# Half of a feed-forward stage's features turned by DMA transposes as pairs of float16 numbers, and 1/std taken for two groups at once

## The chip, the cores and the metric

The kernel runs on one core of a Trainium2 chip. The metric is the device time of one execution in microseconds (us), the median of three runs. A separate, profiled execution gives the page and the trace that are quoted below. Engines: PE is TensorE (PEld its weight loads), DVE is VectorE, ACT is ScalarE, POOL is GpSimd, SP issues transfers.

## The reference

Two layers, each a graph attention followed by a feed-forward part, each with a residual, on x of 4096 x 256 float32 and one 4096 x 4096 adjacency matrix. The change touches the feed-forward part of layer 0 alone, a recurrence of 30 steps on the 4096 rows:

```python
def step(h, _):
    h = h + 0.01 * jnp.tanh(h)
    h = h * jax.nn.sigmoid(h)
    h = _layernorm(h, ln_w, ln_b)
    h = jnp.einsum('bsc,dc->bsd', h, W) + b
    return (h, None)
x, _ = jax.lax.scan(step, x, None, length=N_ITERS)      # N_ITERS = 30
...
x = x + _L0_ffn_ref((_layernorm(x, axis=-1))[None], ...)[0]
```

W is 256 x 256. Each row is independent of the others, so different rows may stand in different steps at the same time, but a row's step needs the result of its step before.

## The kernel before, in words

The kernel is written in a tile framework: the program states operations and the pools from which their buffers come, and the framework puts the operations of each engine into a queue whose order it chooses, and adds the semaphore waits. An engine works through its queue strictly in that order. Stages: attention 0 (to about 842 us), the feed-forward recurrence (842 to about 1921 us), attention 1 with its two layers, a router, and a mixture of experts.

In the feed-forward stage all 4096 rows stay on chip in `y` (128 partitions x 32 row tiles x 256 columns, float32). `y` holds 100 times h, which spares a multiplication. A group is four row tiles (G = 4, 512 rows); there are eight groups (NG = 8). A unit is one group in one step, so there are 30 x 8 = 240 units, and unit u + 8 is the next step of unit u's group. The loop over `at` starts unit `at` and carries earlier units on, so that several are under way:

- unit `at`: L739, ACT, `th = tanh(0.01 y)`, 128 x 1024; L740, POOL, `th = th + y`.
- unit `at - 1`: L745, ACT, `z = silu(0.01 th)`. Then `over_std` (L101 to L106): the row statistics on DVE (four of L101, four of L103), the addition of EPS (L105, DVE) and the power -0.5 (L106, POOL) give 1/std of each row.
- unit `at - 2`: L114, PE, eight transposes of `z` by 128 x 128 into PSUM (`tp`), then L780, ACT, a copy to SBUF (`zT`, 128 x 1024).
- unit `at - 3`: L754, PE, eight float32 products of `zT` with `wT` (W transposed, the layer norm's weight and mean folded in) into `po`; each float32 product is two records in the trace. Then L764, DVE, four times `y = po * (1/std) + bias`.

```python
th[at] = work.tile([P, G, C], F32, name="th")
nc.scalar.activation(th[at], y[:, g * G : (g + 1) * G, :], AF.Tanh, scale=0.01)
nc.gpsimd.tensor_tensor(th[at], th[at], y[:, g * G : (g + 1) * G, :], OP.add)
...
z = zs[at - 1] = work.tile([P, G, C], F32, name="z", bufs=4)
nc.scalar.activation(z, th.pop(at - 1), AF.Silu, scale=0.01)
rs[at - 1] = over_std(small, z)[0]
...
zT[at - 2] = work.tile([P, KC, GR], F32, name="zT")
nc.scalar.copy(zT[at - 2], pt)
```

`th` and `zT` have three buffers each (the pool `f_work`), `z` has four, `po` and `tp` two each in PSUM. In the last step (units 232 to 239) L764 adds `last` in place of `bias`, and L774, DVE, adds the residual. Before the loop, `init` (L679 to L683) normalizes each group of the stage's input, and a preparation (L698 to L721) makes `wT` and `bias`.

Of the kernel before, what the change touches and what calls it, by code (L numbers as in the profile page):

```python
# [11 lines left out]
F32 = mybir.dt.float32  # L12
BF16 = mybir.dt.bfloat16
F16 = mybir.dt.float16
I32 = mybir.dt.int32
AF = mybir.ActivationFunctionType
OP = mybir.AluOpType
AX = mybir.AxisListType
# [3 lines left out]
P = 128  # L22
C = 256
KC = C // P
# [3 lines left out]
G = 4  # L28
EPS = 1e-5
# [6 lines left out]
TINY = 1e-30  # L36
# [8 lines left out]
def gnn_ffn_kernel(ctx: ExitStack, tc: tile.TileContext, a: dict, out: bass.AP):  # L45
    nc = tc.nc
# [3 lines left out]
    NG = NT // G  # L50
    GR = G * P
# [14 lines left out]
    nc.gpsimd.memset(ones, 1.0)  # L66
    lnscale = const.tile([P, 1], F32, name="lnscale")
    nc.gpsimd.memset(lnscale, math.log(SCALE * LOW))
    mhalf = const.tile([P, G], F32, name="mhalf")
    nc.gpsimd.memset(mhalf, -0.5)  # L70


# [23 lines left out]
    def over_std(pool, src):  # L96

        st = pool.tile([P, G, 6], F32, name="ln_st")
        mv = pool.tile([P, G, 2], F32, name="ln_mv")
        for r in range(G):  # L100
            nc.vector.bn_stats(st[:, r, :], src[:, r, :])  # L101
        for r in range(G):
            nc.vector.bn_aggr(mv[:, r, :], st[:, r, :])  # L103
        rstd = pool.tile([P, G], F32, name="ln_rstd")
        nc.vector.tensor_scalar(rstd, mv[:, :, 1], EPS, None, op0=OP.add)  # L105
        nc.gpsimd.tensor_tensor(rstd, rstd, mhalf, OP.pow)  # L106
        return rstd, mv

    def transposed(psum, src, name="tp"):

        ps = psum.tile([P, KC, GR], F32, name=name)
        for k in range(KC):
            for r in range(G):
                nc.tensor.transpose(ps[:, k, r * P : (r + 1) * P], src[:, r, k * P : (k + 1) * P], ident)  # L114
        return ps
# [540 lines left out]

    with ExitStack() as scope:
        one = scope.enter_context(tc.tile_pool(name="f_one", bufs=1))  # L660
        wT = one.tile([P, KC, C], F32, name="wT")
        bias = one.tile([P, C], F32, name="bias")
        last = one.tile([P, C], F32, name="last")
        y = one.tile([P, NT, C], F32, name="y")
        work = scope.enter_context(tc.tile_pool(name="f_work", bufs=3))
        small = scope.enter_context(tc.tile_pool(name="f_small", bufs=6))

        x1 = {}

        def load(g):  # L670
            if g not in ahead:
                load_ahead(x1d, g)
            x1[g] = ahead.pop(g)

        def init(g):
            t = x1.pop(g)
            rstd, mv = over_std(small, t)
            rs = small.tile([P, G], F32, name="rs")
            nc.vector.tensor_scalar(rs, rstd, 100.0, None, op0=OP.mult)  # L679
            nm = small.tile([P, G], F32, name="nm")  # L680
            nc.vector.scalar_tensor_tensor(nm, mv[:, :, 0], -1.0, rs, op0=OP.mult, op1=OP.mult)
            for r in range(G):
                nc.scalar.activation(  # L683
                    y[:, g * G + r, :], t[:, r, :], AF.Identity, scale=rs[:, r : r + 1], bias=nm[:, r : r + 1]
                )

        load(0)
        load(1)
        with tc.tile_pool(name="f_prep", bufs=1) as prep, tc.tile_pool(name="f_pps", bufs=1, space=PSUM) as pps:
            ln = prep.tile([2 * KC, P], F32, name="ln")  # L690
            nc.scalar.dma_start(ln[:KC], a["L0_ffn_ln_w"].rearrange("(k p) -> k p", p=P))
            nc.scalar.dma_start(ln[KC:], a["L0_ffn_ln_b"].rearrange("(k p) -> k p", p=P))
            wr = prep.tile([P, KC, C], F32, name="wr")
            nc.scalar.dma_start(wr, a["L0_ffn_W"].rearrange("(k p) c -> p k c", p=P))
            nc.scalar.dma_start(bias, bcast_rows(a["L0_ffn_b"]))
            init(0)
            ps = pps.tile([P, 2 * KC], F32, name="ps_ln")
            nc.tensor.transpose(ps, ln, ident[: 2 * KC, : 2 * KC])  # L698
            lnT = prep.tile([P, 2 * KC], F32, name="lnT")
            nc.vector.tensor_scalar(lnT, ps, 100.0, None, op0=OP.mult)  # L700
            lbb = prep.tile([P, KC, P], F32, name="lbb")
            nc.vector.tensor_copy(lbb, lnT[:, KC:, None].to_broadcast([P, KC, P]))
            ps = pps.tile([P, KC, C], F32, name="ps_w")
            for k in range(KC):
                for o in range(KC):
                    nc.tensor.transpose(ps[:, k, o * P : (o + 1) * P], wr[:, o, k * P : (k + 1) * P], ident)
            raw = prep.tile([P, KC, C], F32, name="raw")
            nc.vector.tensor_copy(raw, ps)
            ps = pps.tile([P, C], F32, name="ps_b")
            for k in range(KC):  # L710
                nc.tensor.matmul(ps, lbb[:, k, :], raw[:, k, :], start=(k == 0), stop=(k == KC - 1))
            nc.vector.scalar_tensor_tensor(bias, bias, 100.0, ps, op0=OP.mult, op1=OP.add)

            nc.vector.tensor_scalar(last, bias, -100.0, None, op0=OP.add)
            for k in range(KC):
                nc.vector.tensor_scalar(raw[:, k, :], raw[:, k, :], lnT[:, k : k + 1], None, op0=OP.mult)
            ps = pps.tile([P, C], F32, name="ps_m")
            for k in range(KC):
                nc.tensor.matmul(ps, mean, raw[:, k, :], start=(k == 0), stop=(k == KC - 1))
            for k in range(KC):  # L720
                nc.vector.tensor_tensor(wT[:, k, :], raw[:, k, :], ps, OP.subtract)  # L721

        ps_t = scope.enter_context(tc.tile_pool(name="f_pst", bufs=2, space=PSUM))
        ps_o = scope.enter_context(tc.tile_pool(name="f_pso", bufs=2, space=PSUM))

        th, zs, rs, zT = {}, {}, {}, {}
        units = FFN_STEPS * NG
        for at in range(units + 4):
            if at < NG:
                if at + 2 < NG:  # L730
                    load(at + 2)
                if at:
                    init(at)
            if units - NG <= at - 1 < units:
                load((at - 1) % NG)
            if at < units:
                g = at % NG
                th[at] = work.tile([P, G, C], F32, name="th")
                nc.scalar.activation(th[at], y[:, g * G : (g + 1) * G, :], AF.Tanh, scale=0.01)  # L739
                nc.gpsimd.tensor_tensor(th[at], th[at], y[:, g * G : (g + 1) * G, :], OP.add)  # L740
            if 0 <= at - 2 < units:
                pt = transposed(ps_t, zs.pop(at - 2))
            if 0 <= at - 1 < units:
                z = zs[at - 1] = work.tile([P, G, C], F32, name="z", bufs=4)
                nc.scalar.activation(z, th.pop(at - 1), AF.Silu, scale=0.01)  # L745
                rs[at - 1] = over_std(small, z)[0]
            if 0 <= at - 3 < units:
                u = at - 3
                g = u % NG
                src = zT.pop(u)  # L750
                po = ps_o.tile([P, G, C], F32, name="po")
                for r in range(G):
                    for k in range(KC):
                        nc.tensor.matmul(  # L754
                            po[:, r, :],
                            src[:, k, r * P : (r + 1) * P],
                            wT[:, k, :],
                            start=(k == 0),
                            stop=(k == KC - 1),
                        )  # L760
                rstd = rs.pop(u)
                end = u >= units - NG
                for r in range(G):
                    nc.vector.scalar_tensor_tensor(  # L764
                        y[:, g * G + r, :],
                        po[:, r, :],
                        rstd[:, r : r + 1],
                        last if end else bias,
                        op0=OP.mult,
                        op1=OP.add,  # L770
                    )
                if end:
                    t = x1.pop(g)
                    nc.vector.scalar_tensor_tensor(  # L774
                        t, y[:, g * G : (g + 1) * G, :], 0.01, t, op0=OP.mult, op1=OP.add
                    )
                    nc.sync.dma_start(rows_of(x2d, g), t)
            if 0 <= at - 2 < units:
                zT[at - 2] = work.tile([P, KC, GR], F32, name="zT")
                nc.scalar.copy(zT[at - 2], pt)  # L780


# [457 lines left out]
```

## Time and profile before

| | before |
|---|---|
| median of 3 runs | 3596.79 us (3593.67 to 3600.78) |
| profiled execution, span | 3585.3 us |
| PE busy in the span | 3265.5 us (91%) |
| DVE, ACT, POOL busy | 3013.9 (84%), 2612.6 (73%), 1101.1 (31%) |
| L740, the add on POOL | 240 times, mean 2367 ns |
| L739, L745, tanh and silu on ACT | 240 times each, means 1047 and 1060 ns |
| L780, the copy of zT on ACT | 240 times, mean 1012 ns |
| L764, the update of y on DVE | 928 times, mean 468 ns, and 32 in the last step |
| L106, the power on POOL | 272 times, mean 1040 ns |

The page lists, by line of the kernel, an engine's operations with what they write and read, how often, busy time, and the mean length of one. A line of the timeline gives the start in us, the time from the first start to the last end of operations of one kind in a row, the engine, the line, the operation, its output and inputs with their sizes, how many, and in brackets how long the engine stood idle before it and what it waited for. Lengths overlap: the next operation of an engine can start a little before the last one's end, so that costs in a chain are better read from start to start. In the windows each engine has its busy time and, in parentheses, the number of its instructions. PEclk is the granted clock of PE as a share of its full speed.

### The profile page before, as it was taken

How to read it: one execution, taken by the hardware profiler on the slowest of the kernel's cores; microseconds unless marked ns; L12 is line 12 of the kernel's file. 1: busy time of each engine (PE TensorE's matmuls, PEld its weight loads, DVE VectorE, ACT ScalarE, POOL GpSimd, SP SyncE). 2: the span in 40 equal slices, each digit the busy share in tenths (PEclk: the TensorE clock that was granted, in tenths of full speed). 3: DMA queues.
4: the chain of work that ended last, by engine and by line, in shares of the span. 5: the costliest groups of instructions: out<-in, count | busy, mean ns of one | idle time of the engine just before them, and what ended most of it. 6: DMA issues, size and time to landing. Idle time of an engine off the chain costs nothing. (4 is left out here: it accounts for less than half of the span.)

```text
span 3585.3 us, 80790 instructions
## 1 busy us (share of the span) xinstructions
PE 3265.5 (91%) x33523; PEld 2971.2 (83%) x33523; DVE 3013.9 (84%) x6039; ACT 2612.6 (73%) x2902; POOL 1101.1 (31%) x899
## 2 busy tenths in 40 slices
PE   6789999987999999999998899999979999996895
PEld 5688888886888888888887799999868999994784
DVE  6789999987877877877787799999989999997445
ACT  2688888896766666666663799999879999993221
POOL 3210010003877777777772000000000000001663
PEclk8899999998999999999999899999999999998897
DMA  6796877601000000000006021303130331404224
GB/s 136 138 230 118 204 171 152 191 22 54 7 1 1 1 1 1 1 1 1 1 1 213 19 73 68 116 25 116 56 123 26 121 117 37 131 20 165 82 94 183
DMA packets 280199, 288.46 MB, mean 80 GB/s; under 512 B 97149, under 2 KB 230426, under 8 KB 279834
## 3 DMA queue, kind: packets, MB, share of 16 engines
q1 hardware_dynamic: 198770, 224.18, 18.9%
q0 software_dynamic: 73920, 52.97, 9.6%
q10 hardware_dynamic: 7144, 6.16, 0.6%
q8 instruction: 264, 4.33, 0.5%
q14 instruction: 101, 0.83, 0.1%
HBM read 248.01 MB, written 68.81 MB: 88 GB/s over the span
## 5 line engine op out<-in xcount | busy, mean ns | idle before, releaser
L546 PE MATMUL acc<-vals,m 128*128 128x130 f16 (+1 forms) x19456 | 1723.4, 233 | 138.1 <-DVE u L475 81.8
L466 ACT ACTIVATE st<-f1b,f2b 128x1024 bf16<-128x1024 f32 (+2 forms) x1664 | 1658.5, 1072 | 146.1 <-DVE m L580 138.2
L546 PEld LDWEIGHTS <-m 128*128 128x128 bf16 x19456 | 1525.2, 98 | 232.2 <-issue 85.7
L580 DVE TENSOR_TENSOR m<-st,m 128x2048 bf16<-128x2048 bf16 (+2 forms) x832 | 929.3, 1134 | 16.3 <-ACT st L466 12.4
L754 PE MATMUL po<-wT,zT 128*128 128x256 f32 x3840 | 875.2, 381 | 12.7 <-ACT zT L780 12.3
L754 PEld LDWEIGHTS po<-wT,zT 128*128 128x128 f32 x3840 | 714.0, 191 | 103.9 <-ACT zT L780 14.8
L740 POOL TENSOR_TENSOR th<-th,y 128x1024 f32<-128x1024 f32 x240 | 567.9, 2367 | 194.1 <-ACT th L739 193.5
L546 PE MATMUL acc<-vals,rows 128*128 128x130 f16 x5120 | 611.1, 221 | 0.0
L106 POOL TENSOR_TENSOR ln_rstd<-ln_rstd,mhalf 128x4 f32<-128x4 f32 x272 | 282.5, 1040 | 896.4 <-DVE ln_rstd L105 685.8
L101 DVE BATCH_NORM_STATS2 ln_st<-z 128x6 f32<-128x256 f32 x960 | 337.7, 413 | 191.3 <-ACT z L745 191.3
L546 PEld LDWEIGHTS <-rows 128*128 128x128 bf16 x5120 | 490.8, 96 | 0.4
L780 ACT COPY zT<-tp 128x1024 f32<-128x1024 f32 x240 | 243.0, 1012 | 323.8 <-PE tp L114 323.8
L604 DVE TENSOR_TENSOR rows<-m,m 128x2048 bf16<-128x2048 bf16 x320 | 391.7, 1224 | 10.2
L764 DVE SCALAR_TENSOR_TENSOR y<-po,ln_rstd,bias 128x256 f32<-128x256 f32 x928 | 378.2, 468 | 4.9 <-PE po L754 4.9
L745 ACT ACTIVATE z<-th 128x1024 f32<-128x1024 f32 x240 | 254.3, 1060 | 18.1 <-POOL th L740 17.8
L114 PE MATMUL tp<-ident,z 128*128 128x128 f32 x1920 | 250.8, 274 | 9.0 <-ACT z L745 8.0
L114 PEld LDWEIGHTS tp<-ident,z 128*128 128x128 f32 x1920 | 225.6, 141 | 35.7 <-ACT z L745 10.7
L739 ACT ACTIVATE th<-y 128x1024 f32<-128x1024 f32 x240 | 251.1, 1047 | 4.7 <-DVE y L764 4.7
L209 POOL DMA_DIRECT2D rows<-in_adj_dram x80 | 72.9, 912 | 510.1 <-PE tp_m L219 499.8
L604 DVE TENSOR_TENSOR m<-m,m 128x1792 bf16<-128x1792 bf16 (+1 forms) x200 | 202.2, 1011 | 12.7
L449 POOL MEMSET hs<- 128x4 f32 x3 | 0.3, 101 | 617.6 <-DVE u L490 596.4
L307 PE MATMUL ph<-g_w,xT 128*128 128x264 f32 x384 | 117.5, 469 | 31.1 <-DVE v L377 27.9
(212 smaller groups left out, 2312.9 us busy)
## 6 DMA issues: line engine op xcount, KB each, us to landing
m<-edges SPq DMA_DIRECT2D x32, 2048.0 KB, 9.8
rows<-in_adj_dram POOLq DMA_DIRECT2D x64, 448.0 KB, 7.1
edges<-ms SPq DMA_DIRECT2D x64, 448.0 KB, 5.1
m<-edges SPq DMA_DIRECT2D x16, 1792.0 KB
f1b<-fd SPq DMA_DIRECT2D x32, 512.0 KB, 3.5
rows<-x1d SPq DMA_DIRECT2D x16, 512.0 KB, 6.8
y<-yd SPq DMA_DIRECT2D x16, 512.0 KB, 9.0
f1b<-fd SPq DMA_DIRECT2D x16, 448.0 KB, 3.7
```

Of the source, the lines that this page charges most:

```text
L101: nc.vector.bn_stats(st[:, r, :], src[:, r, :])
L106: nc.gpsimd.tensor_tensor(rstd, rstd, mhalf, OP.pow)
L114: nc.tensor.transpose(ps[:, k, r * P : (r + 1) * P], src[:, r, k * P : (k + 1) * P], ident)
L466: nc.scalar.activation(st[:, s, :w], f1b[c, h][:, :w], AF.Relu, bias=f2b[:, 2 * q + s, h : h + 1], scale=BIG)
L546: nc.tensor.matmul(acc[:, i, cols], lhs[:, s, rows], v[:, cols], start=(j == 0 and n_ == 0), stop=(j == NT - 1 and n_ == 1), skip_group_ch ...
L580: nc.vector.tensor_tensor(m1[:, :, :w], st[:, :, :w], m, OP.logical_and if turned(q) else OP.min)
L604: nc.vector.tensor_tensor(m2[:, :, :w], m, m1[:, :, :w], OP.subtract)
L739: nc.scalar.activation(th[at], y[:, g * G : (g + 1) * G, :], AF.Tanh, scale=0.01)
L740: nc.gpsimd.tensor_tensor(th[at], th[at], y[:, g * G : (g + 1) * G, :], OP.add)
L745: nc.scalar.activation(z, th.pop(at - 1), AF.Silu, scale=0.01)
L754: nc.tensor.matmul(po[:, r, :], src[:, k, r * P : (r + 1) * P], wT[:, k, :], start=(k == 0), stop=(k == KC - 1),)
L764: nc.vector.scalar_tensor_tensor(y[:, g * G + r, :], po[:, r, :], rstd[:, r : r + 1], last if end else bias, op0=OP.mult, op1=OP.add,)
```

## The change

The features of a row are 256 columns. Their first half stays as it was: four transposes on PE instead of eight, a copy by ACT of half the size, four float32 products. The second half takes another way. It is scaled by a power of two and split into two float16 numbers, `z16[:, 0]` (rounded, by ACT) and `z16[:, 1]` (what the rounding lost, by DVE); both are turned by one DMA transpose of 128 x 1024 float16 numbers, issued on SP, into `zT16`; and each part is multiplied with two float16 parts of W's second half, `w16`, which makes four products of 128 x 256 per row tile, added up in PSUM with the float32 product. The scales come from the weights and the bias in the preparation; `under` takes them out again. 1/std is taken for two units at once: the statistics of an even and an odd unit go to one tile `mv2`, and one EPS addition, one power and one multiplication with `under` serve both. The products and the update of y move from `at - 3` to `at - 4`; `zT` and the new tiles have four buffers. It is for relieving PE: fewer float32 products and transposes.

The diff, without the preparation of the scales (some twelve small operations on DVE, one power on POOL, and two products on PE, between L721 and the loop), and without the moved load of the last step:

```diff
-        wT = one.tile([P, KC, C], F32, name="wT")
+        wT = one.tile([P, C], F32, name="wT")
+        w16 = one.tile([P, 2, C], F16, name="w16")
+        scale = one.tile([P, 2], F32, name="scale")
+        under = one.tile([P, 2 * G], F32, name="under")
...
             if 0 <= at - 2 < units:
-                pt = transposed(ps_t, zs.pop(at - 2))
+                z = zs.pop(at - 2)
+                pt = ps_t.tile([P, GR], F32, name="tp")
+                for r in range(G):
+                    nc.tensor.transpose(pt[:, r * P : (r + 1) * P], z[:, r, :P], ident)
             if 0 <= at - 1 < units:
-                z = zs[at - 1] = work.tile([P, G, C], F32, name="z", bufs=4)
-                nc.scalar.activation(z, th.pop(at - 1), AF.Silu, scale=0.01)
-                rs[at - 1] = over_std(small, z)[0]
-            if 0 <= at - 3 < units:
-                u = at - 3
+                u = at - 1
+                z = zs[u] = work.tile([P, G, C], F32, name="z", bufs=4)
+                nc.scalar.activation(z, th.pop(u), AF.Silu, scale=0.01)
+                z16 = work.tile([P, 2, G, P], F16, name="z16", bufs=4)
+                nc.scalar.activation(z16[:, 0], z[:, :, P:], AF.Identity, scale=scale[:, :1])
+
+                st = small.tile([P, G, 6], F32, name="ln_st")
+                if u % 2 == 0:
+                    mv2 = small.tile([P, 2 * G, 2], F32, name="mv2")
+                for r in range(G):
+                    nc.vector.bn_stats(st[:, r, :], z[:, r, :])
+                nc.vector.scalar_tensor_tensor(
+                    z16[:, 1], z[:, :, P:], scale[:, :1], z16[:, 0], op0=OP.mult, op1=OP.subtract
+                )
+                zT16[u] = work.tile([P, 2 * G, P], F16, name="zT16", bufs=4)
+                nc.sync.dma_start_transpose(zT16[u], z16.rearrange("p s r c -> p (s r c)"))
+                for r in range(G):
+                    nc.vector.bn_aggr(mv2[:, u % 2 * G + r, :], st[:, r, :])
+                if u % 2 == 1:
+                    both = small.tile([P, 2 * G], F32, name="both")
+                    nc.vector.tensor_scalar(both, mv2[:, :, 1], EPS, None, op0=OP.add)
+                    nc.gpsimd.tensor_tensor(both, both, mhalf, OP.pow)
+                    nc.gpsimd.tensor_tensor(both, both, under, OP.mult)
+                    rs[u - 1], rs[u] = both[:, :G], both[:, G:]
+            if 0 <= at - 4 < units:
+                u = at - 4
                 g = u % NG
-                src = zT.pop(u)
+                src, src16 = zT.pop(u), zT16.pop(u)
                 po = ps_o.tile([P, G, C], F32, name="po")
                 for r in range(G):
-                    for k in range(KC):
-                        nc.tensor.matmul(
-                            po[:, r, :],
-                            src[:, k, r * P : (r + 1) * P],
-                            wT[:, k, :],
-                            start=(k == 0),
-                            stop=(k == KC - 1),
-                        )
+                    nc.tensor.matmul(po[:, r, :], src[:, r * P : (r + 1) * P], wT, start=True, stop=False)
+                    for part in range(2):
+                        for other in range(2):
+                            nc.tensor.matmul(
+                                po[:, r, :],
+                                src16[:, part * G + r, :],
+                                w16[:, other, :],
+                                start=False,
+                                stop=(part == 1 and other == 1),
+                            )
...
             if 0 <= at - 2 < units:
-                zT[at - 2] = work.tile([P, KC, GR], F32, name="zT")
+                zT[at - 2] = work.tile([P, GR], F32, name="zT", bufs=4)
                 nc.scalar.copy(zT[at - 2], pt)
```

## The prediction

> **What bounds the kernel now.** I looked first at the busy slices on the page: the feed-forward stage is the stretch where POOL stands at 7 (about 842 to 1920 us, 1078 us). It has 240 units (30 steps by 8 groups of four row tiles). Then busy time by window inside that stage, then the timeline of one unit.
>
> ```profile
> core 0: us, PE busy (x) PEld busy (x) DVE busy (x) ACT busy (x) POOL busy (x), PEclk, DMA share, GB/s
> 1400.00:1500.00 100.00, 100.00 (x556) 89.27 (x556) 79.75 (x303) 67.03 (x69) 78.19 (x47) 1.00 0.00 1
> ```
>
> PE is busy for all 100 us at full clock, no other engine above 80%, DMA idle. A unit's timeline:
>
> ```profile
> 1402.24 1.06 ACT L745 ACTIVATE z<-th 128x1024 f32<-128x1024 f32 x1
> 1402.53 1.02 POOL L106 TENSOR_TENSOR ln_rstd<-ln_rstd,mhalf 128x4 f32<-128x4 f32 x1
> 1403.19 1.05 ACT L739 ACTIVATE th<-y 128x1024 f32<-128x1024 f32 x1
> 1403.33 1.41 DVE L101 BATCH_NORM_STATS2 ln_st<-z 128x6 f32<-128x256 f32 x4 [0.88 <-ACT z L745]
> 1404.38 2.37 POOL L740 TENSOR_TENSOR th<-th,y 128x1024 f32<-128x1024 f32 x1 [0.84 <-ACT th L739]
> 1404.58 1.04 PE L114 MATMUL tp<-ident,z 128*128 128x128 f32 x8
> 1404.65 0.36 DVE L103 BATCH_NORM_AGGREGATE ln_mv<-ln_st 128x2 f32<-128x6 f32 x4
> 1404.93 1.63 DVE L764 SCALAR_TENSOR_TENSOR y<-po,ln_rstd,bias 128x256 f32<-128x256 f32 x4
> 1405.46 3.62 PE L754 MATMUL po<-wT,zT 128*128 128x256 f32 x16
> 1406.57 1.06 ACT L745 ACTIVATE z<-th 128x1024 f32<-128x1024 f32 x1
> 1408.91 1.04 PE L114 MATMUL tp<-ident,z 128*128 128x128 f32 x8
> ```
>
> PE transposes start at 1404.58, products at 1405.46, the next transposes at 1408.91: 0.88 + 3.45 = 4.33 us a unit, with no gap. So a transpose costs 0.110 us, and each of the 16 records of the 8 fp32 products 0.216 us. 240 x 4.33 = 1039 us. Note also silu at 1406.57: it starts before the POOL add of 1404.38 has ended (1406.75), so it reads an earlier add. That lead of one unit is what keeps POOL's 2.37 us off the path.
>
> **What the Trainium skill says.** (1) "SBUF — State Buffer", section Who interferes with whom: a DVE instruction with two SBUF inputs contends with a GpSimd instruction that reads SBUF, and so does one in a 2-port mode; whichever issues first holds the shared ports for its whole length, the other fully blocks. The trace agrees, in both directions:
>
> ```profile
> 855.06 2.34 POOL L740 TENSOR_TENSOR th<-th,y 128x1024 f32<-128x1024 f32 x1
> 855.12 2.31 DVE L679 TENSOR_SCALAR rs<-ln_rstd 128x4 f32<-128x4 f32 x1 [1.12 <-POOL ln_rstd L106]
> ...
> 1891.56 1.21 DVE L774 SCALAR_TENSOR_TENSOR rows<-y,rows 128x1024 f32<-128x1024 f32 x1
> 1891.73 1.92 POOL L106 TENSOR_TENSOR ln_rstd<-ln_rstd,mhalf 128x4 f32<-128x4 f32 x1
> ```
>
> The tiny DVE operation (0.17 us elsewhere) ends with the add; the power (1.02 us elsewhere) is stretched to 1.92 by a DVE operation with two SBUF inputs. The y update L764, which reads PSUM and SBUF, runs through the add unhindered. (2) "DMA: Bandwidth & Descriptors", Latency and other measured facts: DMA transposes move 261 GB/s, contiguous ones some 350 to 400. No run of before has one. (3) "VectorE: DVE Perf Modes", The three transpose paths: 1309 ns for one 128x128 16-bit DMA transpose.
>
> **The change, part by part.**
>
> PE: four of eight transposes go (0.44 us), four fp32 products stay (8 x 0.216 = 1.73), sixteen fp16 products of 256 columns come in. The attention stage prices those:
>
> ```profile
> 2399.79 0.22 PE L546 MATMUL acc<-vals,rows 128*128 128x130 f16 x1
> 2400.02 0.22 PE L546 MATMUL acc<-vals,rows 128*128 128x130 f16 x1
> ```
>
> Four starts lie between them: 0.0575 us for 130 columns with a weight load each, so 0.113 for 256; 16 x 0.113 = 1.81. Sum 0.44 + 1.73 + 1.81 = 3.98 us: PE alone would save 0.35 a unit, 84 us.
>
> ACT: tanh and silu stay, zT copies half (about 0.58 for 512 PSUM columns, L281), the high half z16 is new: 0.62 us by the 128x512 copy L1122, about 0.5 from start to start. Sum about 3.2; not a bound by itself.
>
> DVE: from start to start, statistics 1.32, aggregates 0.28, y 1.6. New: the low half (`lo`), 0.69 us by L641 (128x512, two SBUF inputs), 0.62 start to start; the EPS add halves. Sum about 3.9.
>
> POOL: add 2.37; one power on 8 columns for two units: between 1.02 (if its cost is fixed) and 2.0 (if per column), plus a 0.25 us product. 3.0 to 3.5 a unit.
>
> DMA: 256 KB a unit. By (2) 0.7 to 1.0 us of transfer; by (3) taken eight times in a row 10.5 us. I take under 4.8 us, since one instruction's 1024 rows can spread over 16 engines and the buffers (four of each kind) allow several us of latency. Both ends stay for the rivals.
>
> So far nothing exceeds 4.33. But the order of the queues does. The built programs' order on ACT, before and after:
>
> ```
> before: silu(k)  tanh(k+2)  zT copy  silu(k+1)  tanh(k+3) ...
> after:  silu(k)  z16(k)  tanh(k+1)  zT copy  silu(k+1)  tanh(k+2)  z16(k+1)  zT copy  silu(k+2) ...
> ```
>
> Before, tanh is one unit ahead of silu in 231 of 240 units; after, in 12. In 228 units the silu needs the tanh just before it in its own queue, and the add between them. Behind that waiting silu on ACT stand z16, the next tanh and the zT copy, so POOL's add is exposed every unit. Working it out from silu start to silu start: silu to tanh 0.95 (1402.24 to 1403.19), tanh to add start 1.19 (to 1404.38), add 2.37, and 0.03 to the silu, from
>
> ```profile
> 843.40 2.38 POOL L740 TENSOR_TENSOR th<-th,y 128x1024 f32<-128x1024 f32 x1 [3.74 <-ACT th L739]
> 845.81 1.06 ACT L745 ACTIVATE z<-th 128x1024 f32<-128x1024 f32 x1 [1.19 <-POOL th L740]
> ```
>
> That is 4.54 us. Where z16 stands between silu and tanh (about half the units, in alternation) it is 0.52 more, 5.06. Mean 4.80, against 4.33: a floor that no faster PE lifts.
>
> The lock comes on top. `lo` has two SBUF inputs. In the units with z16 behind tanh, z16 ends about 1.57 us after tanh starts and the add starts 1.19 after: `lo` always meets a running add and waits for its end; behind it on DVE stand aggregates and y. In the other units it loses where DVE is late. If all lose, DVE does `lo`, aggregates, y and statistics (3.9 us) after each add's end, which fits into 4.80. That holds while y runs four to six units behind `lo`, as it does for roughly the first 140 units. In the last 99 or so the order on DVE is lo(m-1), y(m-7), statistics(m), lo(m), and tanh(m+1) needs y(m-7), as the eight groups come round. Then the cycle closes: end of add, `lo` 0.65, y 1.68, aggregates 0 to 0.2, 0.04 to ACT, tanh to add 1.19, add 2.37: 5.93 to 6.14, mean 6.03. Where `lo` gets in just before the add in one of two units, a pair takes 11.2 (5.6 each). The power for two units, now issued late in POOL's queue just ahead of an add, can push it to 6.5. I take 5.93.
>
> Sum: 12 x 4.33 + 129 x 4.80 + 99 x 5.93 = 52 + 619 + 587 = 1258 us, less 1039: +219. The preparation of the scales (twelve small DVE operations, a power, two matmuls) stands before the first z16 on ACT: about 8 us. The shared 1/std saves an EPS add and a power in each pair, on engines that aren't the bound: nothing; weights hidden. 3597 + 219 + 8 = 3824, say 3825 us.
>
> **Rivals.**
> - Lead lost, lock hidden: 4.80 throughout: 240 x 0.47 = 113, +8: 3718. For it: DVE has slack. Against: y's place behind `lo` late in the stage.
> - The lock closes the cycle from early on: 6.1 throughout: 1464 - 1039 + 8 = +433: 4030. For it: the lock is seen to be total. Against: y's larger distance early.
> - DMA-bound: 10.5 us a transfer in a row: 240 x (10.5 - 4.33) + 8 = +1489: 5086. For it: price (3); against: price (2).
> - Faster: PE stays the bound at 3.98: 3597 - 84 + 8 = 3521. For it: PE is at 100% and every other sum is under 4; the queues would have to keep their lead, and their order says they don't.
>
> **How the numbers follow.** Forecast 0.62, lock hidden 0.14, lock everywhere 0.10, DMA 0.09, faster 0.04, within 0.2% 0.01. The range 3705 to 4040 takes in the first three (0.86) with their unknown costs: power 1.02 to 2.0, `lo` winning or losing. Slower: 0.95.
>
> **What would show it.** Right: in the stage, PE busy well under 100%; silu idle waiting for the POOL add in nearly every unit, some 2 us each; POOL adds at a period of 4.8 early and nearer 6 late; `lo` with mean durations far above 0.69 us, ending with the adds. The PE steps are right if fp16 starts lie 0.11 apart. Wrong: a period of 4.0 with PE at 100%; ordinary `lo` durations; or the first fp16 weight load waiting for the transfer in each unit, with DMA transposes landing at intervals equal to the period.

## The result, and the profile after

| | before | after |
|---|---|---|
| median | 3598.78 us (4 runs: the three above and one more) | 3858.84 us (4 runs, 3857.78 to 3861.44) |
| ratio to before | | 1.0722, 95% interval 1.0702 to 1.0742 |
| span of the profiled execution | 3585.3 us | 3855.5 us |
| POOL's adds of units 0 to 239, first start to last start | 843 to 1889, 1046 us | 840 to 2144, 1304 us |

The kernel is slower by 260 us, and the feed-forward stage by 258: the loss lies in the 240 units. Busy time in three stretches of the stage after (columns as in the prediction's first view):

```profile
core 0: us, PE busy (x) PEld busy (x) DVE busy (x) ACT busy (x) POOL busy (x), PEclk, DMA share, GB/s
1000.00:1100.00 100.00, 70.18 (x471) 54.28 (x470) 100.00 (x229) 55.43 (x67) 53.83 (x33) 1.00 0.24 46
1300.00:1400.00 100.00, 83.53 (x562) 64.68 (x560) 100.00 (x271) 62.72 (x80) 68.65 (x40) 1.00 0.30 54
1900.00:2000.00 100.00, 73.48 (x493) 56.77 (x492) 69.87 (x241) 54.73 (x71) 60.03 (x36) 1.00 0.25 48
```

PE has fallen from 100% to 70 to 84%, at full clock. DVE shows 100% in the first two stretches, though its work is under 4 us a unit: an operation that waits for the ports counts as busy. In the last stretch DVE idles too, so another chain holds there. The page's costliest groups of the changed stage (busy us, mean ns, then idle time before and what ended it; the high and low float16 halves go by the name z):

```profile
L820 PE MATMUL po<-wT,zT 128*128 128x256 f32 x1920 | 603.8, 397 | 297.9 <-DVE y L833 292.1
L783 POOL TENSOR_TENSOR th<-th,y 128x1024 f32<-128x1024 f32 x240 | 574.9, 2397 | 348.8 <-ACT th L782 348.4
L792 ACT ACTIVATE z<-th 128x1024 f32<-128x1024 f32 x240 | 253.6, 1057 | 491.1 <-POOL th L783 436.2
L823 PE MATMUL po<-w,zT 128*128 128x256 f16 x3840 | 582.9, 275 | 0.7 <-DMA zT<-z 0.7
L801 DVE SCALAR_TENSOR_TENSOR z<-z,scale,z 128x512 f16<-128x512 f32 x240 | 331.5, 1381 | 0.4 <-issue 0.2
L811 POOL TENSOR_TENSOR both<-both,mhalf 128x8 f32<-128x8 f32 x120 | 210.7, 1756 | 141.4 <-DVE both L810 140.2
```

Silu (L792) idles 436 us for the POOL add, 1.8 us a unit, as forecast. `lo` (L801) takes 1.38 us on average. PE's products (L820) wait 292 us for y on DVE, not for POOL or ACT; the float16 products (L823) wait 0.7 us in all for the DMA transposes.

The period, from the starts of the POOL adds, shows when each wait rules (before: 4.33 us from unit 30 on):

| units | period after, us | lo, mean us | more than before, us |
|---|---|---|---|
| 0 to 19 | 5.56 | 1.7 | 10 |
| 20 to 49 | 5.94 | 2.6 | 51 |
| 50 to 139 | 5.03 | 1.6 | 63 |
| 140 to 239 | 5.68 | 0.73 | 133 |

In units 20 to 49 the closed cycle stands in the timeline (start, duration; in brackets the idle time before and its releaser):

```profile
1002.16 1.62 DVE L833 SCALAR_TENSOR_TENSOR y<-po,both,bias 128x256 f32<-128x256 f32 x4
1003.70 1.39 DVE L800 BATCH_NORM_STATS2 ln_st<-z 128x6 f32<-128x256 f32 x4
1003.81 1.06 ACT L782 ACTIVATE th<-y 128x1024 f32<-128x1024 f32 x1 [0.72 <-DVE y L833]
1004.95 2.35 POOL L783 TENSOR_TENSOR th<-th,y 128x1024 f32<-128x1024 f32 x1 [3.55 <-ACT th L782]
1005.02 2.83 DVE L801 SCALAR_TENSOR_TENSOR z<-z,scale,z 128x512 f16<-128x512 f32 x1
...
1008.06 0.45 DVE L833 SCALAR_TENSOR_TENSOR y<-po,both,bias 128x256 f32<-128x256 f32 x1
```

The end of y (1003.78) starts two things: tanh, and through it the add 1.17 us later; and the statistics, behind which `lo` stands 1.24 us later. `lo` loses the ports by 0.07 us, each time, and the next y stands behind it.

In units 50 to 139 `lo` is often held too, but tanh has its y in good time there (3.2 us before it starts, in the median), and silu waits for its add in each of the 90 units. What rules is the chain of silu, high half (L794), tanh, add:

```profile
1303.13 1.06 ACT L792 ACTIVATE z<-th 128x1024 f32<-128x1024 f32 x1 [1.40 <-POOL th L783]
1304.22 0.72 ACT L794 ACTIVATE z<-z,scale 128x512 f16<-128x512 f32 x1
1304.85 1.04 ACT L782 ACTIVATE th<-y 128x1024 f32<-128x1024 f32 x1
1305.97 2.35 POOL L783 TENSOR_TENSOR th<-th,y 128x1024 f32<-128x1024 f32 x1 [0.83 <-ACT th L782]
1308.35 1.06 ACT L792 ACTIVATE z<-th 128x1024 f32<-128x1024 f32 x1 [1.99 <-POOL th L783]
```

From silu to silu this is 5.22 us, the median of the 56 units in which the high half stands between silu and tanh; in the other 34 the median is 4.48. From unit 140 on `lo` never meets an add, and the picture is another:

```profile
1903.27 1.06 ACT L792 ACTIVATE z<-th 128x1024 f32<-128x1024 f32 x1 [2.16 <-POOL th L783]
1904.23 1.04 ACT L782 ACTIVATE th<-y 128x1024 f32<-128x1024 f32 x1
1904.36 0.43 DVE L800 BATCH_NORM_STATS2 ln_st<-z 128x6 f32<-128x256 f32 x1 [1.48 <-ACT z L792]
1904.70 0.15 DVE L810 TENSOR_SCALAR both<-mv 128x8 f32<-128x8 f32 x1
1904.94 1.64 POOL L811 TENSOR_TENSOR both<-both,mhalf 128x8 f32<-128x8 f32 x1 [1.70 <-DVE both L810]
...
1906.66 0.20 POOL L812 TENSOR_TENSOR both<-both,under 128x8 f32<-128x8 f32 x1
1906.82 2.35 POOL L783 TENSOR_TENSOR th<-th,y 128x1024 f32<-128x1024 f32 x1
1909.20 1.06 ACT L792 ACTIVATE z<-th 128x1024 f32<-128x1024 f32 x1 [2.85 <-POOL th L783]
```

The EPS add of a pair (L810) has slipped on DVE behind the first statistics of the next unit, which wait for its silu. The power waits for L810 and stands in front of an add in POOL's queue: that add starts 3.55 us after silu instead of 2.14, and the next silu waits for the add. This happens in about every second unit; in the others the high half stands between silu and tanh, as in the stretch before.

The queues themselves change along the stage: on DVE, y runs three units behind `lo` up to unit 62, then four and five, and six from unit 133 on.

So three suspects: the lost lead of tanh on ACT; the port conflict of `lo` with the add; the shared power and its EPS add, late in their queues.

### The profile page after: what moved, and what is told of

It is laid out like the page before. It is cut to its first block, busy times and chain, and to the rows that moved or that the text cites. A ratio compares the mean times of both kernels' runs of the same rounds, so it can differ in the third digit from the quotient of the medians.

```text
span 3855.5 us, 83286 instructions
## 1 busy us (share of the span) xinstructions
PE 3237.9 (84%) x34487; PEld 2823.6 (73%) x34487; DVE 3287.0 (85%) x6175; ACT 2673.4 (69%) x3142; POOL 1098.8 (29%) x900
## 5 line engine op out<-in xcount | busy, mean ns | idle before, releaser
L820 PE MATMUL po<-wT,zT 128*128 128x256 f32 x1920 | 603.8, 397 | 297.9 <-DVE y L833 292.1
L792 ACT ACTIVATE z<-th 128x1024 f32<-128x1024 f32 x240 | 253.6, 1057 | 491.1 <-POOL th L783 436.2
L823 PE MATMUL po<-w,zT 128*128 128x256 f16 x3840 | 582.9, 275 | 0.7 <-DMA zT<-z 0.7
L820 PEld LDWEIGHTS po<-wT,zT 128*128 128x128 f32 x1920 | 292.9, 193 | 359.4 <-DVE y L833 335.1
L823 PEld LDWEIGHTS <-zT 128*128 128x128 f16 x3840 | 378.8, 99 | 164.4 <-issue 3.2
L833 DVE SCALAR_TENSOR_TENSOR y<-po,both,bias 128x256 f32<-128x256 f32 x928 | 382.2, 470 | 0.7 <-PE po L823 0.7
L801 DVE SCALAR_TENSOR_TENSOR z<-z,scale,z 128x512 f16<-128x512 f32 x240 | 331.5, 1381 | 0.4 <-issue 0.2
L106 POOL TENSOR_TENSOR ln_rstd<-ln_rstd,mhalf 128x4 f32<-128x4 f32 x32 | 37.4, 1168 | 851.0 <-DVE ln_rstd L105 664.4
L811 POOL TENSOR_TENSOR both<-both,mhalf 128x8 f32<-128x8 f32 x120 | 210.7, 1756 | 141.4 <-DVE both L810 140.2
L794 ACT ACTIVATE z<-z,scale 128x512 f16<-128x512 f32 x240 | 171.9, 716 | 10.8 <-DMA zT<-z 7.0
```

What stands on the lines that cost most here:

```text
L792: nc.scalar.activation(z, th.pop(u), AF.Silu, scale=0.01)
L801: nc.vector.scalar_tensor_tensor(z16[:, 1], z[:, :, P:], scale[:, :1], z16[:, 0], op0=OP.mult, op1=OP.subtract)
L820: nc.tensor.matmul(po[:, r, :], src[:, r * P : (r + 1) * P], wT, start=True, stop=False)
L823: nc.tensor.matmul(po[:, r, :], src16[:, part * G + r, :], w16[:, other, :], start=False, stop=(part == 1 and other == 1),)
L833: nc.vector.scalar_tensor_tensor(y[:, g * G + r, :], po[:, r, :], rstd[:, r : r + 1], last if end else bias, op0=OP.mult, op1=OP.add,)
```

## The experiments

The ratio is to the kernel before, with its 95% interval. "Lead" means that silu of unit k stands behind tanh of unit k+1. The framework orders the queues of each kernel anew, so a run can differ from the changed kernel in more than its edit; where it matters, this is said.

**1. Lead put back.** A dependency that only orders the queue:

```diff
-nc.scalar.activation(z, th.pop(u), AF.Silu, scale=0.01)
+silu = nc.scalar.activation(z, th.pop(u), AF.Silu, scale=0.01)
+if u + 1 in tanh:
+    behind(silu, tanh[u + 1])
```

> The changed kernel with one thing put back: silu of unit k is made to stand behind tanh of unit k+1 in ACT's queue, so that tanh leads by one unit in 239 of 240 units as it did before the change. Everything is computed. Lost-lead theory: the chain silu, tanh, add goes off the path, silu no longer waits for the add, and the period falls towards PE's 3.98 us: 3500 to 3560 us. Port theory (lo against the POOL add): the closed cycle add, lo, y, tanh, add of 5.93 us needs no silu and stays where DVE is late: 3700 to 3860 us, with lo still far above 0.7 us on average. Late-power theory (one power for two groups, queued ahead of an add): the last 100 units keep 5.6 us, 3750 to 3850 us. I expect 3600: most of it the lead, with some lo still blocked.

Measured: 3817.22 us, ratio 1.0637 (1.0619 to 1.0655). Silu's wait for the add is gone, and little is gained, far from the 3600 expected: the lead alone isn't it.

```profile
L801 ACT ACTIVATE z<-th 128x1024 f32<-128x1024 f32 x240 | 250.1, 1042 | 4.1 <-POOL th L792 3.4
L812 DVE SCALAR_TENSOR_TENSOR z<-z,scale,z 128x512 f16<-128x512 f32 x240 | 373.7, 1557 | 0.0
L821 DVE TENSOR_SCALAR both<-mv 128x8 f32<-128x8 f32 x120 | 130.5, 1087 | 1.8
```

These lines are of this run (the lines are shifted): silu waits 4 us in all where it was 491, `lo` takes 1.56 us on average, and the tiny EPS add (L821) 1.09 us, where the late timeline after shows 0.15. From unit 20 on tanh starts 0.03 us after the end of its y, so the cycle through y rules now. The stage's last 120 units run at 5.46.

**2. The port conflict of lo taken away.**

```diff
-    z16[:, 1], z[:, :, P:], scale[:, :1], z16[:, 0], op0=OP.mult, op1=OP.subtract
+    z16[:, 1], z[:, :, P:], scale[:, :1], zero, op0=OP.mult, op1=OP.mult    # zero: PSUM
```

> The changed kernel, but lo's second input is a constant in PSUM in place of the high half in SBUF, so lo no longer has two SBUF inputs; it leaves out the true low half (the product reads another number). ACT's order keeps tanh without a lead in 229 units. Port theory: lo takes about 0.7 us everywhere, the cycle with y vanishes, units 20 to 49 and 50 to 139 fall to 4.0: 3540 to 3650 us. Lost-lead theory: the floor of 4.54 to 5.06 stays (4.8 on average) in all units: 3855 less 30 x 1.1 less 90 x 0.2 less some of the last 100, so 3690 to 3780 us. Late-power theory: only the last 100 units matter, at 5.66, unchanged: 3800 us. I expect 3720.

Measured: 3630.64 us, ratio 1.0119 (1.0102 to 1.0136). The largest single effect, 228 us off. `lo` takes 0.73 us in every unit, and the period is 4.47 from unit 20 to the end, which is the bare chain: silu 0.97 tanh 1.11 add 2.35 silu 0.04. What the port theory had expected (PE as the bound) didn't come, since the lead is still missing, and neither did the late power's 5.66.

Not all of the 228 us is the conflict, though, because the queues came out differently too: from unit 20 on no high half stands between silu and tanh, y stays three units behind `lo` on DVE to the end, and the EPS add no longer stands behind the next unit's statistics. From unit 140 on, where the changed kernel's `lo` isn't held at all, this run still saves 119 us. In units 20 to 49 DVE's order is the same in both, and there 5.94 falls to 4.47, 44 us: so much the conflict costs there, on top of the chain. Here too the EPS add is stretched:

```profile
1505.32 2.35 POOL L786 TENSOR_TENSOR th<-th,y 128x1024 f32<-128x1024 f32 x1 [0.24 <-ACT th L785]
...
1506.27 1.44 DVE L813 TENSOR_SCALAR both<-mv 128x8 f32<-128x8 f32 x1
...
1507.71 1.06 ACT L795 ACTIVATE z<-th 128x1024 f32<-128x1024 f32 x1 [1.37 <-POOL th L786]
```

It ends at 1507.71, with the add (1507.67), though it has one input and eight numbers per partition.

**3. A power for each unit.**

```diff
-if u % 2 == 1:
-    both = small.tile([P, 2 * G], F32, name="both")
+both = small.tile([P, G], F32, name="both")
```

> The changed kernel with a power on 4 columns for each unit in place of one on 8 columns for two; everything is computed; tanh still has no lead (229 units). Late-power theory: the power no longer waits for the statistics of the next even unit, the add of the last 100 units comes at 2.14 us after silu again instead of 3.55, their period falls from 5.66 to about 4.8: 3760 to 3790 us. Lost-lead and port theories: within 30 us of 3859, or slower by up to 60 us, since POOL gets 1.02 + 0.2 us in each unit in place of 1.64 + 0.2 in two. I expect 3840.

Measured: 3834.64 us, ratio 1.0688 (1.067 to 1.0706). The last 100 units fall from 5.68 to 5.10 us (58 us), as the late-power theory said; but units 20 to 79 now all run at 5.97 (`lo` 2.84), the closed cycle. The net is 24 us (10 in the stage). Sharing the power was no gain in this kernel.

**4. Lead put back and lo without its conflict.** The edits of 1 and 2 together.

> Both edits: tanh led by one unit again, and lo's second input a PSUM constant (the true low half is left out). Lost-lead and port theories together: nothing but PE is left, 3.98 us a unit, 240 x 3.98 = 955 against 1039 before, and 8 for the preparation: 3505 to 3530 us with PE at 100% in the stage. Late-power theory: a power of 1.6 us and an add of 2.37 us in a row on POOL still exceed 3.98 in every second unit, 3600 us or more.

Measured: 3599.19 us, ratio 1.0033 (1.0022 to 1.0045). The late-power theory's number, but run 5 shows that the power isn't the reason: 4.26 us a unit, PE at 95%, DVE at 100%.

```profile
1500.00:1600.00 100.00, 95.39 (x661) 75.97 (x660) 100.00 (x319) 76.22 (x96) 76.80 (x46) 1.00 0.33 62
```

```profile
1504.09 2.36 POOL L795 TENSOR_TENSOR th<-th,y 128x1024 f32<-128x1024 f32 x1 [1.43 <-ACT th L794]
...
1505.46 1.02 DVE L824 TENSOR_SCALAR both<-mv 128x8 f32<-128x8 f32 x1
...
1506.56 1.64 POOL L825 TENSOR_TENSOR both<-both,mhalf 128x8 f32<-128x8 f32 x1
```

The EPS add again ends with the add (1506.45). The Trainium skill says why this can be: "SBUF — State Buffer", section Who interferes with whom, lists `tensor_scalar` among the operations that can enter a 2-port mode and so take the pair shared with GpSimd. The trace agrees: 1.00 us on average here, 1.36 in run 2, 0.15 at the least.

**5. The EPS add moved from DVE to POOL, on top of 4.**

```diff
-nc.vector.tensor_scalar(both, mv2[:, :, 1], EPS, None, op0=OP.add)
+nc.gpsimd.tensor_tensor(both, mv2[:, :, 1], eps8, OP.add)
```

> As the run before it with tanh leading and lo's second input in PSUM (3599 us, 4.26 us a unit), and one edit more: the EPS add of the pair (128x8) moves from DVE to POOL as an addition of a constant tile. The true low half is left out as there. Theory A (the EPS add on DVE is a second victim of the ports: it stood 1.02 to 1.44 us where 0.15 would do, and ended with the POOL add, and DVE is at 100%): DVE falls to about 3.8 us a unit, PE is the bound at 3.98: 3599 less 220 x 0.28 = 3537 us or a little less, PE at 100%. Theory B (4.26 is set by the chain of ACT, or by POOL's power ahead of the add): no change, or 0.1 us a unit slower as POOL has 0.2 us more for each pair, 3595 to 3625. I expect 3540.

Measured: 3517.05 us, ratio 0.9809 (0.9793 to 0.9826). PE is at 100% and the period 3.92: with the three waits gone, PE is the bound, and nothing else stood behind them. The shared power still stands in POOL's queue. Up to unit 69 DVE's order is that of run 4 without the EPS add, and already in units 20 to 49 the mean period falls from 4.26 to 3.84.

```profile
1500.00:1600.00 100.00, 100.00 (x715) 81.79 (x714) 99.08 (x337) 81.02 (x103) 85.51 (x65) 1.00 0.40 70
```

The DMA engines' share is 0.40 here, against 0.24 to 0.30 in the changed kernel, and PE doesn't wait for them.

**6. Everything computed: silu's second half twice.** To stay clear of the ports, `lo` must read one of its inputs from PSUM. ACT computes the second half once more into a PSUM bank, and both halves are made from it; with the edits of 1 and 5.

```diff
+zh = ps_z.tile([P, G, P], F32, name="zh")
+nc.scalar.activation(zh, th[u][:, :, P:], AF.Silu, scale=0.01)
-nc.scalar.activation(z16[:, 0], z[:, :, P:], AF.Identity, scale=scale[:, :1])
+nc.scalar.activation(z16[:, 0], zh, AF.Identity, scale=scale[:, :1])
-    z16[:, 1], z[:, :, P:], scale[:, :1], z16[:, 0], op0=OP.mult, op1=OP.subtract
+    z16[:, 1], zh, scale[:, :1], z16[:, 0], op0=OP.mult, op1=OP.subtract
```

> Everything is computed. The changed kernel with tanh leading, the EPS add on POOL, and the second half of silu computed once more by ACT into a PSUM bank, from which both fp16 halves are made, so that lo reads PSUM and SBUF. ACT gets about 0.5 us a unit more (3.2 + 0.5, from start to start), PE keeps 3.98. If the port conflict on DVE was all that stood above PE: 3520 to 3550 us, faster than before the change. If ACT's longer queue becomes the bound: 3.98 to 4.3 a unit, 3550 to 3610. I expect 3545.

Measured: 3565.67 us, ratio 0.9948 (0.9932 to 0.9965), 0.5% faster than before. The period is 3.92 up to unit 180, then 5.1. The late stretch:

```profile
1804.55 1.06 ACT L794 ACTIVATE th<-y 128x1024 f32<-128x1024 f32 x1
1805.50 1.05 ACT L804 ACTIVATE z<-th 128x1024 f32<-128x1024 f32 x1
1805.68 2.36 POOL L795 TENSOR_TENSOR th<-th,y 128x1024 f32<-128x1024 f32 x1 [2.75 <-ACT th L794]
1808.08 0.60 ACT L808 ACTIVATE zh<-th 128x512 f32<-128x512 f32 x1 [1.52 <-POOL th L795]
```

The new half silu (L808) belongs to the tanh at 1804.55 and waits for its add: the framework had put it one unit earlier. A lead lost again, of another operation.

**7. The lead taken from the kernel before.** The products come one unit later in the program; with them go, as in the change, a fourth buffer for `zT` and the load of the last step one unit later. Nothing else of the change is in it. The main part of the edit:

```diff
-if 0 <= at - 3 < units:
-    u = at - 3
+if 0 <= at - 4 < units:
+    u = at - 4
```

> The kernel before the change with one edit: the products and the update of y come one unit later in the program (four units after tanh instead of three), which alone turns the order on ACT from tanh(k+1) silu(k) to silu(k) tanh(k+1) in 230 of 240 units. Nothing of fp16, DMA or pairs is in it. Lost-lead theory: the chain silu, tanh, add of 4.47 us replaces PE's 4.33, 240 x 0.14 = 34: 3615 to 3630 us; with the EPS add of each unit blocked by the POOL add behind that, up to 3680. Port theory alone: no lo, no change, 3580 to 3600.

Measured: 3647.68 us, ratio 1.0171 (1.0154 to 1.0188). That is more than the 3615 to 3630 expected for a chain of 4.47. The period is 4.54, which is the forecast's chain to the hundredth:

```profile
1502.65 1.06 ACT L745 ACTIVATE z<-th 128x1024 f32<-128x1024 f32 x1 [1.65 <-POOL th L740]
...
1503.62 1.04 ACT L739 ACTIVATE th<-y 128x1024 f32<-128x1024 f32 x1
...
1504.80 2.37 POOL L740 TENSOR_TENSOR th<-th,y 128x1024 f32<-128x1024 f32 x1 [1.06 <-ACT th L739]
```

So the one unit of distance that the change adds, to leave the transposes and the pair time, is enough to turn ACT's order, without the rest of the change. The whole edit costs 60 us; 0.21 us in each of 240 units is 50 of it.

**8. An operation like lo added to the kernel before, its lead kept.**

```diff
+nc.vector.scalar_tensor_tensor(
+    extra, z[:, :, P:], 0.01, z[:, :, :P], op0=OP.mult, op1=OP.subtract
+)
```

> The kernel before the change with one DVE operation added in each unit, of lo's kind and size (128x512, two SBUF inputs, float16 out), which nobody reads; tanh keeps its lead in 231 of 240 units. Nothing else of the change is in it. Port theory: it waits for POOL adds, y falls behind, the closed cycle of up to 5.93 us appears: 3700 to 3900 us, its mean duration over 1.2 us. Lost-lead theory: 0.7 us more on DVE (80 percent busy of 4.33 us, so about 96 percent) stays hidden behind PE: 3585 to 3610 us.

Measured: 3611.51 us, ratio 1.007 (1.0053 to 1.0087). The 24 us fall in the first 40 units (there it takes up to 2.68 us); then the period is 4.33 again, and the operation takes 0.68:

```profile
1503.71 0.68 DVE L748 SCALAR_TENSOR_TENSOR extra<-z 128x512 f16<-128x512 f32 x1
1503.88 1.39 POOL L106 TENSOR_TENSOR ln_rstd<-ln_rstd,mhalf 128x4 f32<-128x4 f32 x1
...
1505.74 2.36 POOL L740 TENSOR_TENSOR th<-th,y 128x1024 f32<-128x1024 f32 x1 [0.47 <-ACT th L739]
```

Here it falls between two adds, and it is the power that waits (1.39 against 1.02 us), which nobody on the path needs. The port theory's 3700 to 3900 was wrong: two inputs in SBUF aren't a cost by themselves, it is where they fall in the cycle. From unit 40 on this operation stands behind y and the EPS add in DVE's queue, not right behind its own statistics as `lo` does, so the run doesn't price `lo` itself.

**9. Run 6 with its order mended.**

```diff
-nc.scalar.activation(zh, th[u][:, :, P:], AF.Silu, scale=0.01)
+half = nc.scalar.activation(zh, th[u][:, :, P:], AF.Silu, scale=0.01)
+behind(half, silu)
```

> Everything is computed. As the run with silu's second half computed twice (3566 us), and that half is made to stand behind the full silu of its own unit in ACT's queue. There, from unit 180 on, it had slipped in front, directly behind the add it needs, and the last 60 units took 5.1 us in place of 3.92. If that slip is the whole loss: 60 x 1.2 = 72 us off at most, but the run with a PSUM constant took 3517, so 3510 to 3530 us, PE at 100% to the end of the stage. If another wait stood there: 3550 to 3570. I expect 3520.

Measured: 3515.01 us, ratio 0.9789 (0.9776 to 0.9803): 2.1% faster than before with everything computed. The period is 3.92 to the end:

```profile
1700.00:1800.00 100.00, 100.00 (x717) 81.94 (x716) 98.53 (x335) 93.16 (x129) 86.13 (x65) 1.00 0.39 67
```

**10. lo with two SBUF inputs, but no wait for the high half.**

```diff
-    z16[:, 1], z[:, :, P:], scale[:, :1], z16[:, 0], op0=OP.mult, op1=OP.subtract
+    z16[:, 1], z[:, :, P:], scale[:, :1], z[:, :, :P], op0=OP.mult, op1=OP.mult
```

> The changed kernel, but lo takes silu's first half (SBUF) as its second input in place of the high half: it keeps two SBUF inputs and no longer waits for ACT's high half. The true low half is left out. It parts what the PSUM constant took away together: the ports, and the wait for the high half, which ends after the POOL add has started. If the ports alone matter: as the changed kernel, 3800 to 3870 us, lo still 1.3 to 2.8 us until unit 140. If it is the wait for the high half that puts lo behind each add: lo near 0.8 us and 3630 to 3720 us. I expect 3780.

Measured: 3860.45 us, ratio 1.0753 (1.0737 to 1.077), as the changed kernel and not the 3780 expected, with `lo` at 2.84 us and 5.94 a unit in units 20 to 49. So it isn't the wait for ACT that holds `lo`, and not what run 2 gained by; what is left of it are the ports, and the order of the queues that came with its edit.

**11. The EPS add moved to POOL, alone.** The edit of 5 in the changed kernel.

> The changed kernel with one edit: the EPS add of the pair moves from DVE to POOL. Everything is computed; tanh has no lead, lo its two SBUF inputs. Late-power theory: in the last 100 units the power waited for that EPS add, which stood behind statistics of the next unit on DVE; without it they fall from 5.66 to about 4.6 to 4.8: 3760 to 3790 us. If the power is late for another reason (the aggregates before it are late too), 3830 to 3870. I expect 3790.

Measured: 3855.31 us, ratio 1.074 (1.0724 to 1.0757): no gain. Units 20 to 39 fall from 5.94 to 4.70, but from unit 120 on `lo` meets every add again, and the period is 5.74:

```profile
1904.84 2.36 POOL L785 TENSOR_TENSOR th<-th,y 128x1024 f32<-128x1024 f32 x1 [0.67 <-ACT th L784]
1904.91 2.83 DVE L803 SCALAR_TENSOR_TENSOR z<-z,scale,z 128x512 f16<-128x512 f32 x1
```

The expectation of 3790 was wrong: the late power went, and `lo` took its place.

**12. Only lo left.** The edits of 1 and 5; everything is computed.

> The changed kernel with tanh leading again and the EPS add on POOL; everything is computed; only lo against the POOL add is left of the three suspects. It differs from the run of 3517 us in lo's second input alone. Port theory: the cycle add, lo, y, tanh, add stays, 5 to 5.95 us a unit: 3700 to 3850 us. If lo's conflict only mattered together with the other two: 3520 to 3580 us. I expect 3740.

Measured: 3626.48 us, ratio 1.0107 (1.0091 to 1.0122): 4.2 to 4.3 us a unit from unit 90 on, with `lo` at 1.1 on average. It costs 109 us against run 5, less than expected: with a lead, `lo` meets an add in 61 of the 240 units.

The medians together, in us:

| lead | lo without conflict | EPS add on POOL | median |
|---|---|---|---|
| no | no | no | 3859 (after) |
| yes | no | no | 3817 |
| no | yes | no | 3631 |
| no | no | yes | 3855 |
| yes | yes | no | 3599 |
| yes | no | yes | 3626 |
| yes | yes | yes | 3517; 3515 with everything computed |

The kernel before was measured anew beside each set of runs, at 3587 to 3599 us, and in the profile after, what follows the stage took 1676 us against 1658 to 1670 in the others; so some 10 us of each difference from 3859 may not be the edit's. In the stage alone, from the first add to the last, the differences are cleaner. The effects don't add: alone the edits bring 42, 228 and 4 us (in the stage 29, 216 and -1), 274 in sum, and together 342 (in the stage 329, where the sum is 244). The EPS add is worth nothing clear of the noise in the changed kernel, and 191 us where the lead is there (3817 to 3626).

## Why the prediction was right, and which steps weren't

The time, 3825 forecast and 3859 measured, and the direction came from the named mechanism: queue order and ports, not the sum of the work. That the number came so close is luck in part. The forecast's loss is 61 us in the first 141 units (129 x 0.47) and 158 in the last 99 (99 x 1.60); measured were 124 in units 0 to 139 and 133 in the last 100, and these by another wait than the one named. By its steps:

- *PE at 3.98 us.* Held, a little high: 3.92 in runs 5 and 9, at 100% busy. In a row tile the float16 products start 0.109 us apart (four in 0.44 us) against 0.113.
- *ACT's order and the chain of 4.54.* Shown. Silu's wait is there in the profile after; run 7 makes the chain alone in the kernel before and gives 4.54, run 2 gives 4.47 (there the add starts 1.11 us after tanh instead of 1.18). With the high half in between it is longer than forecast: 5.22 us after, not 5.06. The high half needs silu's result and starts 1.09 us after it, where tanh starts 0.96 after it, and tanh follows 0.63 later, so that the high half adds 0.76 us and not 0.52. It stood between silu and tanh in 123 units, about half, as forecast. In units 50 to 139 this chain makes a loss of 63 us. Run 2 isn't a measure of the rival "lost lead, lock hidden", put at 3718: with no high half in between, its 3631 stands for the short chain alone.
- *lo against the add, a cycle of 5.93.* Size right, place and share wrong. The cycle runs at 5.94, but in units 20 to 49 and not in the last 99: tanh meets a late y early on, because DVE runs late there (the bracket at 1003.81 shows it), and not by the order in the queue that the forecast read. That order is there (y of unit 150 behind `lo` of unit 156), but those y are done some 2.4 us before their tanh, and `lo` falls between two adds. The closed cycle costs 51 us where the forecast gave `lo` 99 x 1.13 = 112; the last 100 units are slow all the same, by the power.
- *Why lo always meets the add.* Wrong twice: `lo` is held in 110 units and in none from unit 140 on, and it was put down to `lo`'s wait for the high half. Run 10 takes that wait away and `lo` stays at 2.84. The timeline shows the other cause: one event, the end of y, starts both, and the add is 0.07 us ahead.
- *Power of 1.02 to 2.0 us.* 1.64, between the bounds. That it stands late in POOL's queue was named as able to push the cycle to 6.5; in fact it rules every second one of the last 100 units, where no `lo` is blocked: 5.93 us from silu to silu, against 5.39 in those with the high half in between, 5.68 together. Run 3 takes 58 us off there.
- *The EPS add, saved on engines that aren't the bound: nothing.* Missed. The prediction itself quoted a small tensor_scalar that ended with an add, and still priced this one at its undisturbed duration. It is the second victim of the ports: 82 us between runs 4 and 5, though in the changed kernel, where other waits rule, nothing (run 11).
- *DMA under 4.8 us.* Right: a transpose of 256 KB lands in 3.0 us (median), and PE reaches 100% in runs 5 and 9. The rival that took 1309 ns eight times in a row, from the Trainium skill's page "VectorE: DVE Perf Modes", section The three transpose paths, falls: eight in a row at that price would take 10.5 us, more than three times the measured 3.0.
- *The rival "faster", 3521.* The value of the idea was right: 3515 to 3517 once nothing stands in PE's way.

What stays open: why the framework turns ACT's order when the products move by one unit (the order alone was seen), and why it changes the order along the stage, at about the places where the changed kernel passes from one pattern into another. How much of run 2's 119 us from unit 140 on belongs to which difference in the queues wasn't tested.

## What to carry to other kernels

When work leaves the bounding engine, look next at the queues' order and at shared resources, since a loop that was hidden behind 4.33 us of PE has little to spare at 3.92. Mark every DVE operation that takes the ports shared with GpSimd, tiny ones too, and ask which event starts it and which starts the GpSimd operation: if it is the same event, the same one loses in every round, as `lo` did in units 20 to 46; an input in PSUM, or the other engine, takes it out. Effects of such waits don't add, so an edit that brings nothing alone (the EPS add) may be needed for the rest to pay. And before the difference of two kernels is put down to one edit, compare the order of their queues: it may have changed with the edit.

## What the hardware showed that was not expected

- A DVE operation of 8 numbers per partition took up to 2.22 us in the changed kernel, to the end of a running POOL add (0.15 us undisturbed).
- A held DVE operation counts as busy: DVE stood at 100% in runs where its work was under 4 us of 5 to 6.
- A power on 8 columns took 1.64 us on POOL, on 4 columns 1.02: by these two, 0.16 us a column and about 0.4 fixed (an estimate).
- `lo` with its input in PSUM took 0.73 us, as with both in SBUF undisturbed (0.73).
